# Four graph layers on one core: the written-out order of all engines and the buffer slots replaced by another order of the same steps

## The chip, the cores and the metric

The kernel runs on one core of a Trainium2 chip. The metric is the device time of one execution in microseconds (us), the median of several runs. The core's engines are named as in the profile: PE is TensorE (matmuls; PEld its weight loads), DVE is VectorE, ACT is ScalarE, POOL is GpSimd, SP is SyncE, which here does nothing but issue DMAs. Each has a queue of instructions that it takes strictly in order.

## What is computed

x has 128 batches of 128 nodes with 512 features in float32; adj is one 128 x 128 matrix for all of them. Four layers follow each other, each added to its input and normalised over the features:

```python
x = layernorm(x + (norm_adj @ (x @ W0) + bias))          # layer 0, norm_adj = D^-1/2 adj D^-1/2
x = layernorm(x + L1(x, adj, adj, b))                     # layer 1
q, k, v = x @ Wq.T, x @ Wk.T, x @ Wv.T                    # layer 2
rel = adj.T * (q @ k.T);  rel /= norm(rel, rows)
x = layernorm(x + rel @ v)
h = x @ W3;  e = leaky_relu(h @ a1 + (h @ a2).T) * adj    # layer 3
x = layernorm(x + elu(softmax(e) @ h + beta * h))
```

The kernel has nothing of layer 1 but a normalisation that it joins with that of layer 0.

## The kernel before

**Groups and steps.** The 128 batches are 32 groups of 4 (GB). A group's work is cut into some 240 named steps, methods of the class `Group`; each step issues a few instructions on one engine. A step is written `group.step`, and `s.` stands for the setup of constants and weights. Each of the four large products of a group (w: layer 0's x @ W0; z: layer 2's x times the product Wq.T Wk; v: x @ Wv.T; k: layer 3's x @ W3) is done by seven products of half-size blocks instead of eight (`w1` to `w7`), some of them (1, 2, 5, for v and z also 4) cut once more in the same way. That needs sums of blocks of the left operand (done by POOL) and of the weights (done once by DVE), and additions of the results (DVE).

The steps that the text speaks of:

- `y00` to `y11` (L935): norm_adj times a quarter of x, on TensorE, into a PSUM bank; `cy..` (ACT, L579) copies it to SBUF as y_T. `bi..` (POOL, L585) adds the bias to the same quarter of x in place, after the matmuls that read it.
- `sy0` to `sy3`, `ly12`, `ly5` (POOL, L585): the block sums S_y, l_y of y_T. `w1`, `w2`, ..., `w18` (TensorE, L766 for whole blocks, L730 for those cut once more). `bw`, `ew` (ACT L579, DVE L582): additions inside a cut product. `dw1`... (DVE, L582): results added onto x. `stw`, `gw`, `pow`, `apw`: mean, variance and normalisation.
- `xt`, `nt` (DVE, L674): transposes in 32 x 32 squares of x, for layers 2 and 3. `xd`, `nd` (SP, L680): 16 DMAs that put the squares in their places. `lx12`, `sx0`..., `ln12`, `sn0`... (POOL): block sums of what they bring. `z..`, `v..`, `k..`: the products.
- `r`, `rm`, `sq`, `rp`: rel and its norm. `rt` (DVE) transposes rel by squares, `wr` (SP, L703) writes it to DRAM as d_r, and `cr` (SP, L707) reads it back as relT in four DMAs. `f` (TensorE, L1190) multiplies relT and v, and `fa` (DVE, L1199) adds the result to x.
- `sc` (DVE, L1214), `pw`, `pe` (SP): the attention scores; `pl`, `ej`, `ei`, `ex`, `rd`, `so`: their softmax. `at` (DVE), `aw` (SP, L703, d_a), `cat` (SP, L707, attT) transpose it as above; `h` (TensorE, L1190) multiplies attT and the product k; `em`, `ee`, `ea` do the elu. `qk`, `gk`, `pok`, `apk`: normalisation. `fin` (SP) writes the output; `ld` (SP) loads a group's x.
- Setup: `s.adjt` (TensorE, L822, L823) transposes norm_adj and adj; `s.warm` (TensorE, L833) does 11 transposes of the identity whose result nobody reads; `s.m012_0` and the like (DVE) are sums of weight blocks.

**What sets the order.** Nothing is scheduled by a compiler. The steps are issued in the order of three strings: HEAD (L110 on) once; TURN (L258 on) 14 times, each time with the group numbers one higher, the last group entering with 11 to 24; TAIL (L275 on) once. Inside a turn some five groups are in work at a time. Every engine takes its own instructions in that order, and waits for the other engines and for DMAs by semaphores. An engine that waits holds back all that stands behind it in its queue.

**Buffers.** Each tile with one of nine tags (bank: six PSUM banks; S, l1, l2: block sums; C: products; aT: transposed operands; m: 128 x 512 tiles such as rel, relT, e, attT; x; q) gets the slot that the string SLOTS names for its turn in the list (L47 on, class `Slotted`). A tile waits until all readers of the tile before it in its slot are done.

```python
for base, steps in (
    [(0, HEAD)] + [(g - BACK, TURN) for g in range(FIRST, end, STEP)] + [(end - BACK, TAIL)]
):
    for group, name in (t.split(".") for t in steps.split()):
        todo[group if group == "s" else base + int(group)].step(name)
```

Of the kernel before, what the change touches and what calls it, by code (L numbers as in the profile page):

```python
# [48 lines left out]
        "012345012345013324015345231455124240510435012532245312312023543413421402402052145230142402"  # L49
        "405233100340153013205320521340135305355234252351453524503210430454115310512125312305211451"  # L50
        "412523102304253042541105305015021541030340351405232432352315320142424230314525325435403451"
        "025252541243050250302310324152525234530121521015041053425252503201454254142134120352525210"
        "514323523435403451025252541243050250302310324152525234530121521015041053425252503201454254"
        "142134120352525210514323523435403451025252541243050250302310324152525234530121521015041053"
        "425252503201454254142134120352525210514323523435403451025252541243050250302310324152525234"
        "530121521015041053425252503043201513105140152035033042453510140541524513202020314220445020"
        "545523405212550033235143024014515313210213142055015354151041043201425125523020130023054354"
        "2045151501250312315415401340132145131523152403145324501324051324051"
    ),
    "S": (  # L60
        "012345601326054321502461532143250123654012106425231064104632501462035142560413524651203546"
        "413406524103561463205164231534062135410216534012605403216504352651403256124320651423046145"
        "320641563062145360231534062135410216534012605403216504352651403256124320651423046145320641"
        "563062145360231534062135410216534012631450326154036413652014326504152602324316052432560324"
        "152630645016325064152306"
    ),
    "l1": (
        "010111010101010010101011001101001011010010110100101101001011010010110100101101001011010010"
        "110100110010110011010110100100110"
    ),  # L70
    "l2": (
        "010101010101010010110110110110110110110110110110110110110110110110110110110110110101110101"
        "01"
    ),
    "C": (
        "010101010101011010101011011011011011011011011011011011011011011011011011011011011011011010"
# [3 lines left out]
        "012100212102102012012102012102012102012102012102012102012102012102012102012102102012012010"  # L80
        "2110210"
    ),
    "m": (
        "012301202302301210320100130133212013131201310310213231201012103232120131323021213103232120"
        "131323021213103232120131323021213103232120131323021213103232120131323021213103232120131323"
        "02121310233221302022132020213201210312121203210030"
    ),
    "x": (
        "0123457869789012345768901234576890123457689012345768901234576981032"
    ),  # L90
    "q": (
        "010101010101010001001010101010101010101010101011010101010101010100101010101001010101010101"
        "010101010101010001010101010101010101010101010101010101010101010101010101010101010101010101"
        "010101010101010101010101010101010101010101010101010101010101010101010101010101010101010101"
        "010101010101010101010101010101010101010101010101010101010100010101010101010101010101010101"
        "01010101010101010101010101010101010101010101010101010101010101010101010"
# [14 lines left out]
0.ld1 2.ld0 0.ld0 2.ld1 1.ld1 1.ld0 s.warm s.deg s.root s.nadj s.adjt s.nadjT 0.y10 0.y01 0.cy10  # L111
1.y10 0.cy01 1.y11 1.cy10 1.y01 1.cy11 0.y11 s.m012_0 1.cy01 3.ld1 s.s00 0.w2 s.m012_1 0.cy11
s.s02 0.bi10 s.m012_3 0.y00 0.bi01 2.y10 s.s01 0.cy00 2.y11 0.bi00 0.w1 s.m05_0 0.sy0 s.s03 2.y00
1.y00 0.bi11 s.m05_1 1.cy00 0.sy2 s.m012_2 0.w5 1.bi10 s.m05_3 0.sy3 0.dw1 s.m05_2 0.w6 0.sy1
0.dw2 s.sk0 1.ly12 s.sk2 s.g1 0.dw6 s.s30 0.w7 s.cg1 1.sy0 s.m312_0 1.bi11 0.dw7 s.m312_1 0.w4
1.bi00 0.dw5 s.bi 0.w3 s.sa1 2.cy10 0.dw4 2.cy00 s.sk1 2.cy11 s.g2 s.sa0 0.dw3 0.stw3 3.y11 1.bi01
0.stw0 s.g5 0.stw1 s.sa2 s.dg2 2.y01 s.s31 1.sy2 0.stw2 1.w2 2.cy01 s.s33 s.g6 0.gw s.sa3 1.bw2
s.m35_0 1.w1 s.cg6 0.pow 1.ew2 s.g7 1.bw1 s.m35_1 2.bi11 1.ew1 0.apw0 0.apw1 1.w28 0.xt0 1.ly5
1.w18 s.cg7 s.sk3 s.la 0.apw2 0.apw3 1.sy1 1.w5 1.dw1 3.ld0 0.xt2 s.g4 1.bw5 0.xt1 2.bi01 0.xt3
s.q11 1.w6 2.bi00 s.cg4 0.xd 1.ew5 s.mg12_0 3.bi11 1.w58 s.dg5 s.q02 s.g3 2.bi10 1.dw6 1.dw2 1.w7  # L120
s.dg3 2.ly12 s.mg12_1 1.dw7 s.mg12_3 1.w4 s.sg0 1.dw5 s.sg2 2.w2 s.sg1 4.ld0 2.w1 s.m312_3 2.bw2
s.sg3 2.ew2 2.bw1 0.z1 0.sx0 s.vt3 s.vt0 0.sx2 s.vt1 2.w28 0.cz1 1.dw4 1.sy3 s.vt2 0.z6 1.stw3
s.vd 0.sx1 1.stw2 1.w3 0.cz6 0.sx3 s.mg4_0 2.sy0 0.z5 2.ew1 1.dw3 2.sy1 0.z7 s.mg4_1 2.ly5 1.stw1
2.w18 s.mg4_3 0.cz7 0.z2 2.sy2 0.dz5 1.stw0 0.z4 0.dz2 1.gw s.mg5_0 s.mg12_2 1.pow s.mg5_2 0.z3
0.cz4 s.mg5_1 s.m35_3 1.apw3 s.mg5_3 3.y10 2.dw1 1.apw2 s.sv0 0.v1 1.apw0 3.bi10 2.dw2 1.apw1
1.xt2 s.sv1 0.v2 0.cv1 1.xt3 0.dz3 0.v6 1.xt0 0.dv2 1.xt1 0.r0 s.sv3 0.cv6 1.xd s.mv5_0 2.w5
s.mv4_0 s.mv5_1 s.mv4_1 s.sv2 0.r1 2.bw5 s.mv4_3 s.mv12_0 0.r2 2.ew5 0.r3 s.mv12_2 s.mv12_1 2.w58
s.mv5_3 s.mv12_3 0.rm 0.v7 s.q10 0.sq0 0.rt 0.sq1 2.w6 0.sq2 s.q12 0.cv7 s.q03 0.sq3 s.q00 0.rp
0.v4 s.q13 0.v5 3.cy11 s.q01 3.cy10 0.wr 2.dw6 0.cv4 4.ld1 3.sy0 s.wt0 s.s32 2.w7 2.sy3 0.cr 0.dv5
s.wt1 s.mv5_2 3.y00 1.sx0 2.dw7 0.v3 s.mg4_2 3.cy00 1.lx12 2.dw5 2.w4 s.mv4_2 0.dv3 0.f3 2.dw4  # L130
3.sy1 0.f1 2.stw2 0.f2 3.bi00 2.stw3 1.v1 0.fa3 1.lx4 0.fa2 1.z1 1.bv1 0.fa1 2.w3 1.bz1 1.ev1
1.lx5 1.ez1 0.f0 1.sx2 1.v5 2.dw3 0.fa0 1.z18 1.sx3 1.bv5 2.stw0 1.v18 0.mnv 1.cz1 1.ev5 1.z5
1.sx1 0.qv2 1.z6 2.stw1 0.qv1 1.cv1 0.qv0 1.z2 1.cz6 1.v6 1.bz2 0.qv3 1.ez2 1.bz5 1.z7 0.gv 2.gw
1.ez5 0.pov 1.cv6 2.pow 1.z28 0.apv3 1.z4 1.cz7 1.dz2 0.apv0 1.z58 0.nt3 2.apw0 1.v2 0.sc00 2.apw2
0.nt0 3.y01 1.bz4 0.sc01 0.apv2 1.v58 3.bi01 1.ez4 3.cy01 1.v7 0.apv1 0.nt2 3.ly5 2.apw1 0.sc10
1.bv2 1.z48 2.apw3 0.nt1 1.v4 1.cv7 3.ly12 1.dz4 0.nd 1.ev2 3.w5 1.bv4 1.dz5 1.v28 3.bw5 0.sc11
1.z3 3.ew5 1.dv2 3.w1 0.sc20 3.w2 1.dz3 3.bw1 0.sc21 3.w58 3.ew1 1.r0 1.r1 0.sc30 3.bw2 1.ev4 1.r2
1.r3 3.ew2 1.v48 0.sc31 3.w18 1.dv4 3.w28 0.pw 3.dw1 1.rm 0.k2 0.sn0 3.dw2 1.sq0 2.xt1 1.sq1 0.sn2
0.pe 2.xt0 0.k1 1.sq2 2.xt2 1.sq3 0.sn3 2.xt3 0.k5 1.rt 0.ck1 2.xd 1.rp 1.dv5 s.m312_2 0.sn1 0.pl3
0.dk2 1.v3 0.pl0 s.m35_2 0.pl1 0.pl2 3.sy2 0.k6 1.dv3 0.ej 3.w6 0.ck6 3.sy3 0.ei 0.ex0 0.k7 3.dw6  # L140
0.ex3 0.ex2 0.ex1 3.w7 0.rd 0.ck7 0.so0 0.dk5 0.so1 4.y11 3.dw7 1.wr 0.k4 3.dw5 4.bi11 0.at 0.aw
2.lx12 3.w4 4.cy11 1.cr 0.ck4 3.w3 3.dw4 2.sx0 3.stw2 0.cat 2.z1 3.stw3 2.sx2 2.z2 3.dw3 2.bz1
3.stw0 1.f2 2.sx1 2.bz2 3.stw1 2.v1 2.lx5 2.ez2 1.f0 3.gw 0.k3 1.fa2 2.bv1 3.pow 1.fa0 2.ez1 1.f1
2.lx4 3.apw0 0.dk3 1.f3 3.apw3 3.xt0 3.apw1 2.z18 1.fa1 3.apw2 0.h0 1.fa3 2.cz1 2.v5 3.xt2 1.mnv
3.xt1 0.h3 1.qv0 2.ev1 2.z28 1.qv1 2.z6 3.xt3 1.qv2 2.dz2 3.xd 1.qv3 0.em3 2.v18 0.em0 2.bv5 1.gv
0.h1 2.cz6 2.ev5 1.pov 0.ee0 2.z7 0.ee3 0.em1 1.apv3 0.ea0 1.apv0 0.ea3 2.v58 2.cz7 2.z5 1.sc00
0.ee1 1.apv1 4.y00 1.sc01 2.bz5 0.ea1 4.y10 1.apv2 4.bi00 2.ez5 4.cy00 4.y01 4.cy10 4.bi10 1.sc10
0.h2 4.cy01 1.sc11 2.z4 4.bi01 2.cv1 0.em2 2.v2 1.sc20 2.bz4 4.sy0 0.ee2 2.z58 2.ez4 2.bv2 2.v6
4.ly12 2.ev2 1.nt1 2.z48 2.cv6 1.sc21 2.v28 2.dz4 2.sx3 2.v7 1.sc30 3.sx0 2.dz5 4.w1 1.sc31 2.cv7
3.lx12 2.dv2 2.z3 1.pw 4.bw1 1.nt2 4.ew1 2.v4 2.dz3 1.pe 4.w18 3.sx2 1.nt0 2.bv4 2.r0 1.nt3 3.lx5  # L150
4.dw1 2.r1 2.ev4 3.z2 4.sy2 0.ea2 2.r2 1.pl3 1.pl0 2.r3 4.sy1 0.mnk 1.pl2 4.w6 1.pl1 3.sx1 2.rm
0.qk3 2.rt 2.sq0 1.ej 2.v48 0.qk2 2.wr 4.dw6 3.z1 2.dv4 1.nd 2.sq1 3.lx4 0.qk1 4.w7 1.ei 2.dv5
3.bz1 1.ex0 3.ez1 1.ex1 2.v3 1.ex3 4.sy3 1.ex2 4.dw7 2.sq2 3.bz2 1.rd 2.sq3 1.so0 3.z18 3.ez2
# [1254 lines left out]
```

## Time and profile before

| what | value |
|---|---|
| median of 3 runs | 1981.98 us (1981.17 to 1983.0) |
| profiled execution | 1983.26 us |
| its span | 1981.5 us, so 1.76 us lie around it |
| granted TensorE clock | 0.998 |
| busy: PE, DVE, POOL, ACT | 1954.1, 1645.2, 1372.1, 1125.0 us |
| first and last matmul | 1.43 and 1969.43 us |
| w0 (first weight) landed | 12.75 us |

How to read the profile: times in the trace are us from the start of the span. A line of the timeline has start, duration, engine, source line and operation, output and inputs, shapes and count; in brackets the idle time before it and what ended it. A line of the waits gives engine and instruction, what it waited for, us in total, times, and the longest. A line of the windows gives the stretch and its length, then busy us and number of instructions of each engine, the granted clock, the busy share of the DMA engines and GB/s. Matmuls are pipelined: a duration of one includes its way through the array, so gaps are measured from start to start.

### The profile page before, as it was taken

The page shows a single profiled execution, that of the slowest core. Times are in us where ns is not written, and L with a number is a line of the kernel's source. Part 1 is how long each engine was busy: PE and PEld are TensorE (multiplying, and loading weights), DVE is VectorE, ACT ScalarE, POOL GpSimd, SP SyncE. Part 2 cuts the span into 40 slices and gives each one's busy share as a digit, 9 for nine tenths or more (in the row PEclk, how much of TensorE's full clock was granted, in tenths as well). Part 3 has the DMA queues.
Part 4 walks back from the last instruction along what each step waited for, and adds up shares of the span by engine and source line. Part 5 has one row for each costly group of instructions (what it writes and reads, how often), then busy time and mean ns, then how long its engine had stood idle before and what let it go on. Part 6 is the DMA issues. An engine that isn't in the chain of part 4 may idle for free.

```text
span 1981.5 us, 37439 instructions
## 1 busy us (share of the span) xinstructions
PE 1954.1 (99%) x12405; PEld 1723.5 (87%) x12405; DVE 1645.2 (83%) x3801; ACT 1125.0 (57%) x2800; POOL 1372.1 (69%) x1702
## 2 busy tenths in 40 slices
PE   8999999999999999999999999999999999999997
PEld 7888988888888988888988888988889888898885
DVE  7888787888788888888888888888888888787887
ACT  2245556565655656565556556556656556566467
POOL 7557678676687776786766776766877767777652
PEclk9999999999999999999999999999999999999999
DMA  5523455334444345444345443445343454434434
GB/s 199 85 52 66 96 80 135 60 87 101 106 100 95 66 89 107 104 99 76 81 91 113 98 106 58 92 98 112 92 102 59 92 106 100 96 62 107 76 73 107
DMA packets 737312, 184.55 MB, mean 93 GB/s; under 512 B 689376, under 2 KB 689760, under 8 KB 737120
## 3 DMA queue, kind: packets, MB, share of 16 engines
q1 hardware_dynamic: 736976, 182.03, 43.7%
q8 instruction: 100, 1.64, 0.4%
q14 instruction: 92, 0.75, 0.1%
q10 hardware_dynamic: 144, 0.13, 0.0%
HBM read 64.03 MB, written 49.87 MB: 57 GB/s over the span
## 4 chain that ended last, share of the span: by engine, by line
PE 86%; SPq 4%; POOL 3%; DMA 2%; DVE 2%; ACT 1%; issue 1%; POOLq 0%; DVEq 0%; ACTq 0%
PE p_w L766 10%; PE p_k L766 10%; PE p_v L730 9%; PE p_z L730 8%; PE p_v L766 8%; PE p_z L766 8%; PE p_w L730 7%; PE p_k L730 6%; PE pr L1142 5%; PE pl_k L1190 5%; PE pl_v L1190 5%; PE py L935 5%; SPq L680 4%; POOL x L585 1%; PE pk L1059 1%
## 5 line engine op out<-in xcount | busy, mean ns | idle before, releaser
L1029 ACT ACTIVATE x<-x,nb,r 128x512 f32<-128x512 f32 x383 | 289.6, 808 | 28.8 <-POOL nb L585 28.5
L585 POOL TENSOR_TENSOR x<-x,bias_bc 128x512 f32<-128x512 f32 x128 | 165.7, 1299 | 122.0 <-PE py L935 92.3
L588 POOL TENSOR_TENSOR r<-v,minus_half 128x4 f32<-128x4 f32 (+1 forms) x99 | 99.1, 1001 | 200.8 <-ACT v L1025 189.5
L582 DVE TENSOR_TENSOR x<-p_w,x 128x512 f32<-128x512 f32 x224 | 153.6, 686 | 48.4 <-PE p_w L766 22.3
L1214 DVE SCALAR_TENSOR_TENSOR e<-x,wa_bc 128x512 f32<-128x512 f32 x256 | 172.3, 673 | 1.4 <-ACT x L1029 0.7
L579 ACT COPY C_k<-p_k 128x512 f32<-128x512 f32 x124 | 71.7, 579 | 150.0 <-PE p_k L766 137.5
L935 PE MATMUL py<-nadjT,x 128*128 128x128 f32 x1024 | 134.8, 277 | 1.0 <-DVE x L1310 0.6
L935 PEld LDWEIGHTS py<-nadjT,x 128*128 128x128 f32 x1024 | 126.9, 193 | 5.1 <-issue 1.4
L1190 PE MATMUL pl_k<-C_k,attT 128*128 128x512 f32 x248 | 122.9, 594 | 1.8 <-DMA attT<-d_a 1.7
L1190 PE MATMUL pl_v<-C_v,relT 128*128 128x512 f32 x248 | 121.0, 593 | 0.9 <-DMA relT<-d_r 0.9
L766 PE MATMUL p_z<-S_x,gq 128*128 128x256 f32 x512 | 121.3, 380 | 0.2 <-DVE C_z L582 0.2
L766 PE MATMUL p_w<-w,S_y 128*128 128x256 f32 x512 | 121.2, 379 | 0.4 <-DVE x L582 0.4
L766 PE MATMUL p_v<-wvT,S_x 128*128 128x256 f32 x512 | 121.1, 379 | 0.0
L1305 ACT ACTIVATE pl_k<-pl_k 128x512 f32<-128x512 f32 x127 | 73.4, 581 | 80.3 <-DVE x L1302 79.4
L766 PE MATMUL p_k<-w,S_n 128*128 128x256 f32 x496 | 117.3, 379 | 0.0
L1199 DVE SCALAR_TENSOR_TENSOR x<-pl_v,r,x 128x512 f32<-128x512 f32 x128 | 94.7, 746 | 23.9 <-PE pl_v L1190 18.9
L582 DVE TENSOR_TENSOR p_z<-p_z,q_z 128x128 f32<-128x128 f32 x248 | 107.3, 433 | 8.5
L582 DVE TENSOR_TENSOR p_v<-p_v,q_v 128x128 f32<-128x128 f32 x248 | 107.3, 433 | 8.5
L766 PEld LDWEIGHTS p_z<-S_x,gq 128*128 128x128 f32 x512 | 94.2, 190 | 21.2 <-issue 6.9
L582 DVE TENSOR_TENSOR C_v<-p_v,C_v 128x512 f32<-128x512 f32 x127 | 86.5, 681 | 28.9 <-ACT C_v L579 13.5
L766 PEld LDWEIGHTS p_w<-w,S_y 128*128 128x128 f32 x512 | 93.2, 190 | 12.2 <-issue 1.1
L766 PEld LDWEIGHTS p_k<-w,S_n 128*128 128x128 f32 x496 | 91.6, 190 | 14.0 <-issue 2.9
(1627 smaller groups left out, 6246.6 us busy)
## 6 DMA issues: line engine op xcount, KB each, us to landing
x<-in_x_dram SPq DMA_DIRECT2D x64, 512.0 KB, 4.5
out_dram<-x SPq DMA_DIRECT2D x127, 256.0 KB, 2.5
d_r<-ru SPq DMA_DIRECT2D x31, 256.0 KB, 2.0
relT<-d_r SPq DMA_DIRECT2D x124, 64.0 KB, 2.5
s<-d_s SPq DMA_DIRECT2D x31, 256.0 KB, 3.8
d_a<-au SPq DMA_DIRECT2D x31, 256.0 KB, 2.3
attT<-d_a SPq DMA_DIRECT2D x124, 64.0 KB, 4.0
w<-in_L_gnn_weight_dram SPq DMA_DIRECT2D x1, 1024.0 KB, 9.5
```

What stands on the lines that cost most here:

```text
L582: nc.vector.tensor_tensor(o, a, b, f)
L585: nc.gpsimd.tensor_tensor(o, a, b, f)
L588: nc.gpsimd.tensor_tensor(o, v, minus_half[:, : v.shape[-1]], ALU.pow)
L680: nc.sync.dma_start(out=o[rows(to), :, :, rows(q)], in_=self.u[rows(q), :, :, to])
L730: nc.tensor.matmul(self.banks[i][:, r, bass.ts(c, P)], lhsT=lhsT, rhs=rhs, start=(not then and n == 0), stop=(n == len(steps) - 1), skip_g ...
L766: nc.tensor.matmul(ps[:, j, :], lhsT=lhsT, rhs=rhs, start=(i not in ONTO and j == 0 and kc == 0), stop=(j == 1 and kc == 1), skip_group_ch ...
L935: nc.tensor.matmul(o, lhsT=self.x_chunk(b, kc), rhs=nadjT, start=True, stop=True)
L1029: nc.scalar.activation(xt, xt, AF.Identity, bias=self.nb[k][:, b : b + 1], scale=self.rstd[k][:, b : b + 1],)
L1142: nc.tensor.matmul(self.pr[:, b, :], lhsT=self.whole["z"][:, fc, b // 2, bass.ts(b % 2, P)], rhs=self.xT.chunk(b, fc), start=(fc == 0), st ...
L1190: nc.tensor.matmul(ps, lhsT=left[:, b, :], rhs=self.whole[k][:, b, :], start=True, stop=True)
L1199: nc.vector.scalar_tensor_tensor(xt, self.pf[b], self.rnorm[:, b : b + 1], xt, ALU.mult, ALU.add, accum_out=self.total("v", b),)
L1214: nc.vector.scalar_tensor_tensor(wide(self.e), self.x(b), 1.0, wide(wa_bc[k]), ALU.mult, ALU.mult, accum_out=self.s[:, k, b : b + 1],)
```

## The change

Only the strings change: SLOTS, HEAD, TURN and TAIL. HEAD, TURN and TAIL hold 2333, 240 and 2040 steps after, 2332, 240 and 2041 before; over the whole program each step occurs as often as before, 7733 in all. No function changes. The order of steps is another one in many places on all five queues. Cut to the places that the text speaks of:

```diff
 HEAD = """
-0.ld1 2.ld0 0.ld0 2.ld1 1.ld1 1.ld0 s.warm s.deg s.root s.nadj s.adjt s.nadjT 0.y10 0.y01 0.cy10
-1.y10 0.cy01 1.y11 1.cy10 1.y01 1.cy11 0.y11 s.m012_0 1.cy01 3.ld1 s.s00 0.w2 s.m012_1 0.cy11
+2.ld1 2.ld0 0.ld0 0.ld1 1.ld0 1.ld1 s.deg s.root s.nadj s.adjt s.warm s.nadjT 0.y01 1.y10 0.cy01
+0.y10 1.cy10 1.y11 0.cy10 1.y01 1.cy11 s.m012_0 3.ld1 s.s00 0.w2 1.cy01 s.m012_1 s.s02 0.bi01
...
-2.sc20 3.v48 5.cy11 5.bi11 4.ew5 1.k7 2.nd 5.sy0 3.dv4 2.sc21 4.w58 1.ck7 5.sy1 3.dv5 1.k28 4.dw5
-5.y01 1.ln5 1.dk2 4.w3 4.stw2 5.cy01 4.stw3 5.ly12 3.v3 2.sc30 4.dw3 2.sc31 3.f2 4.stw1 5.bi01
-5.w1 3.dv3 3.f3 3.fa2 5.bw1 4.stw0 3.f1 3.fa3 1.k5 4.gw 2.pw 5.ew1 4.pow 3.f0 1.bk5 3.fa1 5.w2
-2.ln12 4.apw3 3.fa0 2.pe 5.w18 4.apw0 1.ek5 1.cat 1.k4 3.mnv 5.bw2 4.xt3 3.qv0 5.ew2 2.sn0 1.k58
-3.qv3 2.k1 5.dw1 1.ck4 1.sn3 1.dk5 2.pl3 5.w28 2.pl1 4.xt0 2.k2 3.qv1 5.sy2 5.dw2 1.k3 3.qv2 2.sn1
+4.dw3 2.apv1 2.nt3 3.v3 1.ck7 2.nt2 2.nt1 2.sc01 1.k5 2.nt0 5.y11 1.bk5 1.at 3.cr 2.nd 3.f2 1.ek5
+5.cy11 5.bi11 3.f3 3.fa2 5.sy0 1.k58 3.dv3 3.fa3 3.f0 5.sy1 1.dk5 3.f1 2.sc10 1.k4 3.fa0 2.sc11
+4.stw0 5.y01 1.ck4 2.sc20 5.cy01 5.bi01 4.stw1 2.sc21 4.gw 5.ly12 3.fa1 2.sc30 3.mnv 3.qv0 1.aw
+2.sc31 3.qv3 4.pow 2.pw 5.w1 3.qv1 2.ln12 4.apw0 5.w2 4.apw1 2.pe 4.xt0 1.cat 3.qv2 4.xt1 5.bw2
+3.gv 2.sn0 5.ew2 4.apw2 2.k1 5.bw1 4.apw3 4.xt2 1.sn3 5.w28 2.bk1 5.ew1 2.k2 2.pl3 2.sn2 2.pl1
+2.ek1 1.k3 2.pl2 2.bk2 2.pl0 2.sn1 2.ek2 1.h2 5.sy2 1.dk3 5.w18 4.xt3 3.pov 1.h0 1.em2 4.xd 5.dw1
...
 TURN = """
-4.w1 3.xd 2.cv7 0.qk1 4.w2 4.ly5 2.dv4 4.bw1 1.k1 2.dv5 0.qk3 4.ew1 1.k2 4.bw2 0.gk 1.pl0 0.pok
+4.w1 3.xd 0.qk3 2.dv4 4.ly5 4.w2 4.bw1 2.dv5 0.qk1 1.k1 4.ew1 4.bw2 2.v3 0.gk 0.pok 4.ew2 1.bk1
...
-4.w5 1.aw 2.fa2 5.ld0 4.w7 5.ld1 4.bw5 2.mnv 3.sx0 4.ew5 2.qv0 1.cat 3.z1 2.qv2 4.dw7 3.sx1 4.w58
+2.qv1 1.rd 5.ld1 4.ew5 5.ld0 4.w7 2.qv3 1.ck6 1.so0 2.gv 3.z1 4.dw7 2.pov 4.w58 3.bz1 1.so1 4.w4
+3.ez1 2.apv3 2.apv2 2.nt3 3.sx0 2.apv1 3.z18 1.at 2.apv0 1.k7 4.dw5 3.sx1 1.aw 3.cz1 2.nt1 2.nt0
+3.sx2 1.k28 4.dw4 1.ck7 4.w3 2.nt2 3.lx5 1.cat 1.dk5 1.dk2 1.k4 4.stw2 3.sx3 4.dw3 2.nd 3.lx4
...
```

## Prediction

> **What bounds the kernel now.** I read the page first, then TensorE's waits, then windows of 62 us, then the timeline where the order changes.
>
> ```profile
> span 1981.5 us, 37439 instructions
> ...
> PE 1954.1 (99%) x12405; PEld 1723.5 (87%) x12405; DVE 1645.2 (83%) x3801; ACT 1125.0 (57%) x2800; POOL 1372.1 (69%) x1702
> ...
> PE   8999999999999999999999999999999999999997
> ```
>
> TensorE is full in all slices but the first and the last. Its matmuls start every 111, 216 or 429 ns (128, 256 or 512 columns); all 12405 at that pitch come to 1937.7 us. The first starts at 1.43, the last at 1969.43: 30 us of holes, and a tail of 12. The change keeps every step, so 1937.7 stays; only holes can change.
>
> ```profile
> core 0: us, PE busy (x) PEld busy (x) DVE busy (x) ACT busy (x) POOL busy (x), PEclk, DMA share, GB/s
> ...
> 186.00:248.00 62.00, 62.00 (x429) 57.19 (x428) 48.37 (x111) 31.50 (x88) 42.52 (x53) 1.00 0.35 82
> 248.00:310.00 62.00, 61.22 (x369) 51.91 (x368) 54.24 (x133) 33.86 (x82) 49.55 (x66) 1.00 0.53 103
> 867.00:928.00 61.00, 61.00 (x399) 54.28 (x398) 51.69 (x120) 36.16 (x92) 44.14 (x57) 1.00 0.45 94
> ```
>
> By start-to-start gaps the holes are 11.9 us before 62, 3.1 in the next window, 1.3 and 0.2 in the two after; from 560 to 1700 there are none (a turn takes 60.07 us, its matmuls at pitch 60.2 by my count). So the steady turn has nothing to give; whatever the change gains lies in HEAD and TAIL. The waits name the removable part:
>
> ```profile
> PE p_w L766 <- DVE x L582: 3.8, 4, 1.7
> PE pl_k L1190 <- DMA attT<-d_a: 1.7, 2, 1.4
> ...
> PE p_z L766 <- DMA x_0T<-sq_x: 1.2, 1, 1.2
> PE pl_v L1190 <- DMA relT<-d_r: 0.9, 1, 0.9
> ```
>
> **Gains: the landings.** In starts, the attT waits are 1.6 us (489.0, group 5) and 0.5 (551.2, group 6). At 470.8 to 481.9 SP issues the 16 DMAs of n_6T, group 5's d_a write is issued only at 482.0 though its data was ready at 480.0, and h waits until 490.7. The new order gives group 5 10.6 us from `at` to `h` by its list (8.0 before), and group 6's d_a no longer stands behind squares: -2.1. By the same count n_0T gets 13.1 us instead of 11.35 (needed: 13.3, below): -0.5 of 0.7; relT of group 0 6.8 instead of 6.1: -0.7 of 1.1; x_0T 6.6 instead of 5.9: -0.6 of 1.4. Together **-3.9**. The holes from 290 to 348 (2.7, on POOL, DVE and banks) are reordered: between 0 and -2.7, I take **-1.3**.
>
> **Price 1: the entry to group 5's w product.** This is the large term.
>
> ```profile
> 244.08 11.64 SPq L680 DMA_DIRECT2D n_2T<-sq_n  x16
> ...
> 246.90 1.06 PE L935 MATMUL py<-nadjT,x 128*128 128x128 f32 x8
> ...
> 248.89 1.42 POOL L585 TENSOR_TENSOR l_y<-y_5T 128x256 f32<-128x256 f32 x2
> ...
> 250.26 0.73 POOL L585 TENSOR_TENSOR l_y<-l_y,y_5T 128x256 f32<-128x256 f32 x1
> ...
> 252.33 0.61 PE L730 MATMUL p_w<-m,l_y 128*128 128x128 f32 x4
> ...
> 257.42 1.42 POOL L585 TENSOR_TENSOR l_n<-n_2T 128x256 f32<-128x256 f32 x2 [1.54 <-DMA d_s<-s]
> ```
>
> Step 5.y01 is the matmuls at 246.90; copy, l_y on POOL, then 5.w1 at 252.1, with 4.3 us of other matmuls between. In the new HEAD `5.y01` and `5.w1` are neighbours on TensorE (lead 0; in the turn 13.4), and on POOL bias 5.bi01 stands ahead of 5.ly12. The second matmul of w1 needs the third l_y: y01 1.06, semaphore 0.1, bias 1.27 (as at 251.76), l_y 1.42 and 0.73, so 4.5 us after y01's start, against 1.0 unstalled: **3.5 late**.
>
> Then 2.k1. In the list before, 14.9 us of matmuls lie between 2.nd and it; now 8.5. The row says what is needed: first of 16 issues at 244.08, l_n at 257.42, 13.3 us. Laying the new list's matmuls end to end (list time; trace time is about 43 more), nd can start at 207.3 when the last transpose is done, l_n at 220.6, its third operation ends at 222.8, and k1's second matmul has its place at 216.9: 5.9 late. Behind these three l_n operations POOL has 2.sn0 (1.28) and then 1.sn3 (1.29), for which 1.k3 waits: 222.8 + 2.6 and the handovers give 226.0, place 219.1: **6.9 late**. The three are nested: each absorbs the lateness of the one before. Price +6.9; from 6 to 8 if it all stands, 0 if that work would have been late anyway (rival B).
>
> **Price 2: the start.**
>
> ```profile
> 1.43 2.61 PE L833 MATMUL pt_warm<-ident 128*128 128x128 f32 x11 [1.43 <-POOL ident masks.py:199]
> ...
> 5.64 6.95 PE L935 MATMUL py<-nadjT,x 128*128 128x128 f32 x48 [0.45 <-DVE nadjT L826]
> 12.86 1.32 PE L766 MATMUL p_w<-w,y_0T 128*128 128x256 f32 x5 [0.28 <-DMA w<-in_L_gnn_weight_dram]
> ```
>
> The 11 warming transposes lay in dead time; now they follow the two transposes of nadj, so y starts at 4.98 + 11 x 0.213 = 7.3, not 5.64, and five blocks (4.5 us at full speed) instead of six precede the first w product, which w0's landing holds to 12.8. Does warming pay there? The row: after all transposes y still ran at 213 ns a matmul until 8.15, 2.5 us, 1.25 of it lost. [...] I take the row: 0.2 late, and 0.9 for the sixth block done later. DVE is 97% busy from 12.75 to 70 and sets the pace there, so about half is hidden: **+0.5** (0 to 2.4).
>
> DVE's own order: three sums of weight blocks (2 to 4.6 us) now stand before the work for 0.z1, where before they came after. TensorE already waits for DVE in this stretch: **+1.5** (0 to 3).
>
> **Price 3: small leads.** `4.z6` stands directly behind `4.z18` (copy 0.59, handover 0.27), and some bank and sum leads in HEAD fall: **+1.5** (0 to 4, no row of before shows them). Tail: neighbours are exchanged, both signs, 1 us; 0.
>
> **The turn**, run 14 times. SP's order there changes: loads of group 5 stand before d_a instead of between d_a and attT. Shortest new leads: relT to f 6.8 us, needed 5.1 (four issues 2.6, landing 2.5); squares to l_n 12.8 against 13.3, but k1 has 10 us more; s to pl 4.4. All hold by list: 0, and each 0.1 missed costs 1.4.
>
> **Sum.** -3.9 - 1.3 + 6.9 + 0.5 + 1.5 + 1.5 = +5.2. The profiled execution took 1983.26 (span 1981.5 and 1.76 around it), 1.3 above the median, so I put the sum on the median: 1981.98 + 5.2, about **1987.0**.
>
> **Rivals.** A, the forecast: 1984.5 to 1989.5, 0.47.
> B, on the other side: the 6.9 is a loan. In 186 to 248 TensorE has no hole but POOL and DVE are behind it, and the 2.7 us of holes at 290 to 348 show that they would have stopped it soon; then standing still at 258 only lets them catch up, and the landings' 3.9 and the start's prices remain: 1981.98 - 3.9 - 2.7 + 2.5 = 1978. It decides if the late work refills within one turn. For it: DVE at 54 of 62 us after 248. Against: 2.7 of holes can repay at most 2.7 of 6.9. 0.15.
> C: in addition the turn gets a wait. One of 0.3 us, 14 times, is 4.2: 1991. For it: SP's new order and the lead of 6.8. Against: slack of 1.7 there. 0.11.
> D: the price is half as large (POOL reaches 5.bi01 early, or squares start before 207.3), so that gains and prices cancel: 3.5 instead of 6.9 gives 1983.6; with the small leads at 0, 1982 to 1983. That the landings were corrected and nothing else matters falls here. 0.27.
>
> 0.2% is 4.0 us, about what a measurement of this kernel can tell from no change: under 1978.0 faster, over 1986.0 slower. Of A 0.41 lies above, of C 0.11; of B nearly all lies below: slower 0.52, faster 0.14, same 0.34. The range leaves out B's lower end and C's upper, and reaches over D and A: 1980.5 to 1992.5.
>
> **What would show it.** TensorE waits at p_w for l_y near 258 and at p_k for l_n, then S_n, soon after; their sum 6 to 8. No wait of pl_k for attT near 490 and 551. The first py at 7.3. Windows from 560 to 1700 full. If the window 248 to 310 is as full as before, price 1 is wrong; if the turns are over 60.1 us, C holds.

## The result, and the profile after

The changed kernel took 1990.92 us (median of 5 runs, 1989.78 to 1992.29), the one before 1981.98 (5 runs): ratio 1.0046, 95% interval 1.0031 to 1.0060, so 6 to 12 us slower. Its profiled execution took 1991.07 with a span of 1989.3; that of before 1983.26 and 1981.5. The traces therefore differ by 7.8 us, and these are accounted for below.

The page after, beside the rows shown of before: the busy times of the engines are nearly the same, only the span is longer.

```profile
span 1989.3 us, 37384 instructions
...
PE 1955.8 (98%) x12405; PEld 1725.7 (87%) x12405; DVE 1639.1 (82%) x3801; ACT 1130.1 (57%) x2800; POOL 1368.5 (69%) x1702
```

Two of the three windows after. The turn (867 to 928) is full as before; in 248 to 310 TensorE is busy 56.33 us instead of 61.22, and its granted clock is 0.94 instead of 1.00, which is new:

```profile
core 0: us, PE busy (x) PEld busy (x) DVE busy (x) ACT busy (x) POOL busy (x), PEclk, DMA share, GB/s
248.00:310.00 62.00, 56.33 (x321) 48.47 (x320) 53.66 (x129) 34.48 (x80) 43.24 (x55) 0.94 0.51 92
867.00:928.00 61.00, 61.00 (x397) 54.25 (x396) 50.09 (x118) 35.60 (x89) 44.00 (x57) 1.00 0.43 91
```

TensorE's waits after. The l_y of POOL, 0.2 us before, leads the list; 3.2 of its 5.8 us stand at the place that was forecast, 2.0 near 56 us:

```profile
PE p_w L730 <- POOL l_y L585: 5.8, 3, 3.2
...
PE p_k L730 <- POOL l_n L585: 1.6, 1, 1.6
PE pl_k L1190 <- DMA attT<-d_a: 1.1, 1, 1.1
...
PE pl_v L1190 <- DMA relT<-d_r: 1.0, 2, 0.6
```

**Where the time came from.** Both programs do the same matmuls, so the two traces can be laid on each other by work done: the time at which TensorE has behind it the same us of matmuls at full pitch (the transposes of the setup left out), after minus before. The last digit of these readings is rough.

| work done | time before | after is later by |
|---|---|---|
| 20 us | 31.1 | -0.2 |
| 60 | 76.3 | 2.6 |
| 140 | 158.6 | 1.2 |
| 230 | 248.5 | 2.8 |
| 260 | 278.9 | 10.5 |
| 350 | 372.0 | 10.7 |
| 550 | 574.8 | 9.2 |
| 1935 | 1961.5 | 8.9 |

After the last matmul it is 10.8 us to the end instead of 12.0, which gives back 1.2. So: 2.6 from the start, of which 1.4 are regained by 140 and 1.6 lost again by 230; 7.8 at one place of 30 us; 1.6 regained after it, and 1.2 at the end. The place is the one that was forecast. TensorE's timeline there after:

```profile
260.04 1.05 PE L935 MATMUL py<-nadjT,x 128*128 128x128 f32 x8
260.93 0.39 PE L730 MATMUL p_w<-w,y_5T 128*128 128x128 f32 x2
264.55 0.71 PE L730 MATMUL p_w<-m,l_y 128*128 128x128 f32 x4 [3.23 <-POOL l_y L585]
...
266.63 0.63 PE L730 MATMUL p_k<-w,n_2T 128*128 128x128 f32 x2
268.84 1.22 PE L730 MATMUL p_k<-m,l_n 128*128 128x128 f32 x4 [1.58 <-POOL l_n L585]
```

Step 5.y01 starts at 260.04, w1's second matmul at 264.55: 4.5 us later, as worked out. But compare the durations: four matmuls with l_y show 0.71 at 264.55, four with l_n 1.22 at 268.84. Between these the clock fell. A view of short windows shows it best (last columns: granted clock, DMA share, GB/s):

```profile
261.00:264.50 3.50, 0.32 (x3) 0.12 (x2) 3.27 (x10) 2.41 (x8) 3.32 (x4) 1.00 0.64 91
264.50:265.50 1.00, 0.95 (x8) 0.95 (x9) 0.00 (x0) 0.97 (x3) 0.93 (x2) 1.00 0.83 208
265.50:268.80 3.30, 1.76 (x10) 1.47 (x9) 1.36 (x2) 2.49 (x7) 3.07 (x5) 0.54 0.17 52
268.80:272.00 3.20, 3.16 (x13) 2.92 (x14) 2.82 (x9) 3.20 (x10) 3.14 (x3) 0.50 0.83 151
272.00:276.00 4.00, 4.00 (x22) 3.32 (x22) 2.99 (x9) 1.27 (x4) 4.00 (x5) 0.93 0.01 2
```

TensorE stands still for 3.4 us, works at full speed for 1.2, and then gets half the clock from 265.7 to 272.6, 6.8 us, although it has work for all of that time but the second wait of 1.9. Half the clock for the other 4.9 us costs some 2.5, and 3.4 + 1.9 + 2.5 makes the 7.8.

### The profile page after: what moved, and what is told of

It is laid out like the page before. It is cut to its first block, busy times and chain, and to the rows that moved or that the text cites. A ratio compares the mean times of both kernels' runs of the same rounds, so it can differ in the third digit from the quotient of the medians.

```text
span 1989.3 us, 37384 instructions
## 1 busy us (share of the span) xinstructions
PE 1955.8 (98%) x12405; PEld 1725.7 (87%) x12405; DVE 1639.1 (82%) x3801; ACT 1130.1 (57%) x2800; POOL 1368.5 (69%) x1702
## 4 chain that ended last, share of the span: by engine, by line
PE 92%; DVE 2%; SPq 2%; DMA 1%; POOL 1%; ACT 1%; issue 0%; DVEq 0%; POOLq 0%; ACTq 0%
PE p_k L766 11%; PE p_w L766 10%; PE p_z L730 9%; PE p_v L730 9%; PE p_v L766 9%; PE p_z L766 8%; PE p_k L730 7%; PE p_w L730 7%; PE pr L1142 6%; PE pl_v L1190 5%; PE pl_k L1190 5%; PE py L935 5%; DMA a_bc<-in_L_gnn_a_dram 1%; SPq L680 1%; PE pk L1059 0%
## 5 line engine op out<-in xcount | busy, mean ns | idle before, releaser
L579 ACT COPY C_z<-p_z 128x512 f32<-128x512 f32 x97 | 56.3, 580 | 97.3 <-PE p_z L766 89.7
L579 ACT COPY q_z<-p_z 128x256 f32<-128x256 f32 x124 | 45.9, 370 | 115.2 <-PE p_z L730 106.3
L766 PEld LDWEIGHTS p_v<-wvT,S_x 128*128 128x128 f32 x512 | 93.3, 190 | 13.7 <-issue 2.2
```

The lines of the kernel that those rows point to most:

```text
L579: nc.scalar.copy(o, i)
L766: nc.tensor.matmul(ps[:, j, :], lhsT=lhsT, rhs=rhs, start=(i not in ONTO and j == 0 and kc == 0), stop=(j == 1 and kc == 1), skip_group_ch ...
```

## The experiments

Theory: the change pays at one place for a lead that its list lacks (l_y, then l_n behind it, nested), and for standing still with half a clock; the start costs something more; the landings give back little. Rivals: the wait is a loan that other engines pay back; the waits add up instead of nesting; the clock has nothing to do with them; the landings are late by traffic and not by the queue. "Before" and "changed" below name the two kernels; ratios are to the kernel before, run in the same session. Each trace is of one execution.

**1. The place alone, put into the kernel before** (b_y01). HEAD of before (two bank slots are exchanged with it):

```diff
-5.y01 1.ln5 1.dk2 4.w3 4.stw2 5.cy01 4.stw3 5.ly12 3.v3 2.sc30 4.dw3 2.sc31 3.f2 4.stw1 5.bi01 5.w1
+1.ln5 1.dk2 4.w3 4.stw2 4.stw3 3.v3 2.sc30 4.dw3 2.sc31 3.f2 4.stw1 5.y01 5.cy01 5.bi01 5.ly12 5.w1
```

> The kernel before with one thing of the change: 5.y01 stands directly ahead of 5.w1 on TensorE, and 5.bi01 ahead of 5.ly12 on POOL. Theory (the place costs what its lead lacks): w1's second matmul waits 3.4 us for l_y near 255, and TensorE's granted clock falls to about 0.5 for 3 to 7 us after it, which costs 1.5 to 3 more; 2.k1 has lead enough not to wait. Time +5 (1985.5 to 1988.5). Rival (a loan): POOL and DVE catch up meanwhile, and the holes from 290 to 348, 2.7 us in the kernel before, are gone: +1 to +2.5.

Measured: 1986.51, ratio 1.0020 (1.0011 to 1.0029), +3.9. In its trace TensorE is 0.7 early at 225 us of work, 6.0 late at 245 and 5.2 at 300: in this execution one missing lead costs 6.7, of which 0.8 are paid back. The wait itself is half of it:

```profile
255.37 1.23 PE L730 MATMUL p_w<-m,l_y 128*128 128x128 f32 x4 [3.22 <-POOL l_y L585]
...
256.82 3.62 PE L1190 MATMUL pl_v<-C_v,relT 128*128 128x512 f32 x4
```

Four matmuls of 512 columns take 3.62 us; at full clock the same row is 1.88 before. The price is no loan: 5.6 us of it are there at 1935. The traced execution, 1988.88 us at a mean granted clock of 0.996, is the second slowest of 11; the two at 0.998 took 1984.91 and 1985.41, and the trace of the kernel before, also at 0.998, has full clock all the way from 8.1 to 1974.2 us. So by estimate from these times the wait alone costs some 2.5 us, and the half clock, where it falls, as much again or more.

**2. The place repaired for w1 only** (a_y01). The changed HEAD, with y01 in another free bank:

```diff
-3.dv5 2.apv3 1.k7 2.sc00 2.apv2 4.dw3 2.apv1 2.nt3 3.v3 1.ck7 2.nt2
+3.dv5 2.apv3 1.k7 5.y01 2.sc00 2.apv2 4.dw3 2.apv1 2.nt3 3.v3 1.ck7 5.cy01 5.bi01 5.ly12 2.nt2
```

> The changed kernel with 5.y01, 5.bi01 and 5.ly12 moved some 10 us of TensorE work earlier. Theory (nested waits): w1 waits no more, but the squares of n_2T are issued when they were, so 2.k1 now waits 5 us instead of 1.9 for l_n, the clock falls after it as it did, and the time stays within 1 us (1990 to 1991). Rival (the waits add up): -3.4 and the clock stays full after 1.9 us: -6, 1985.

Measured: 1992.42, ratio 1.0049 (1.0035 to 1.0063): nothing gained. w1 runs through, its 3.4 us stop is gone, and 2.k1 takes all of it back:

```profile
261.48 0.39 PE L730 MATMUL p_w<-w,l_y 128*128 128x128 f32 x2
264.77 0.46 PE L730 MATMUL p_k<-w,n_2T 128*128 128x128 f32 x2 [2.90 <-DMA n_2T<-sq_n]
266.91 1.23 PE L730 MATMUL p_k<-m,l_n 128*128 128x128 f32 x4 [1.68 <-POOL l_n L585]
```

2.90 and 1.68 us, and half clock (1.23 for four matmuls) with the second. The waits are nested: the squares of n_2T and the sums behind them set the price, whether or not w1 waits.

**3. TensorE kept working through both waits** (a_busy). The first matmul of each of the two products is done again and again, into the same place with the same values:

```diff
+BUSY = {("w_5", 1): 14, ("k_2", 1): 11}
-            for n, (r, c, a, b) in enumerate(steps):
+            again = 0 if then else BUSY.get((self.name, i), 0)
+            for n, (r, c, a, b) in enumerate(steps[:1] * again + steps):
+                n = max(0, n - again)
```

> The changed kernel with the first matmul of w1 of group 5 repeated 14 times and that of k1 of group 2 repeated 11 times, into the same place with the same result, so that TensorE works through both waits instead of standing still. Theory (the half clock is the price of standing still for 3.4 us): granted clock 1.0 from 261 to 277; l_n and S_n still come when they come, so that of some 2.5 us at half clock only about 1 is gained: 1990. Rival (the clock would have fallen anyway): matmuls at 213 ns from 265.8 as before, 1991 or later.

Measured: 1990.25, ratio 1.0035 (1.0023 to 1.0048). The clock does not fall:

```profile
262.00:266.00 4.00, 3.87 (x34) 3.68 (x34) 0.86 (x4) 3.11 (x8) 3.71 (x7) 1.00 0.48 108
266.00:268.00 2.00, 2.00 (x20) 2.00 (x19) 1.71 (x3) 2.00 (x6) 1.92 (x3) 1.00 0.65 100
268.00:270.00 2.00, 1.31 (x12) 1.15 (x11) 1.93 (x5) 2.00 (x5) 2.00 (x3) 1.00 0.99 162
```

Without the repeated work, TensorE passes the place 0.9 us less late than in the changed kernel: 6.9 instead of 7.8. So here it is standing still that takes the clock (0.50 from 265.7 to 272.6 in the changed kernel, 1.00 with the repeated work), and of the some 2.5 us that the half clock costs only 0.9 are gained, since l_n and the sums behind it come no earlier. It could not have been earlier: S_n for 1.k3, the last of the three nested terms of the forecast, ends at 270.65, just ahead of the product that reads it:

```profile
269.36 1.29 POOL L586 TENSOR_TENSOR S_n<-n_1T,S_n 128x512 f32<-128x512 f32 x1
270.71 1.99 PE L769 MATMUL p_k<-w,S_n 128*128 128x256 f32 x8
```

**4. The start: single parts undone in the changed kernel.** a_sums moves eight sums of weight blocks behind 0.z7; a_ly2 moves `2.ly12` ahead of `2.bi01`; a_warm moves `s.warm` ahead of `s.deg`.

> The changed kernel with its eight early sums of weight blocks for g and layer 3 (mg5, mg4, m35) put behind 0.z7 on DVE, as they mostly stood in the kernel before. Theory (DVE sets the pace from 45 to 70): the 2.9 us by which TensorE is later there than in the kernel before shrink by 2 to 3: 1988.5. Rival (POOL's l_y and the bias of groups 1 to 3 set it): within 0.7: 1990.5.

> The changed kernel with 2.ly12 ahead of 2.bi01, 2.bi10 and 3.bi11 on POOL (three biases of 1.27 us and more each), since TensorE waits 2.15 us at 56.3 for that l_y: the new order asks for 2.w2 before 1.w7 and 1.w4, the one before after them. Theory (the early loss of 2.7 us is POOL's l_y): no wait at 56, TensorE 1.5 to 2.5 earlier at 100: 1989. Rival (DVE sets the pace there): other waits grow by as much, within 0.5: 1990.7.

> The changed kernel with the 11 warming transposes back ahead of the transposes of norm_adj. Theory (the start is set by the landing of w0 and then by DVE): y starts at 5.6 instead of 7.3, TensorE stands before w0 or later for DVE, and is no earlier at 30: 1990.9 within 0.5. Rival (the transposes cost what they last): 1.5 to 2 earlier for good: 1989.2.

Measured: a_sums 1991.18 (ratio 1.0039, 1.0026 to 1.0053), a_ly2 1990.99 (1.0044, 1.0031 to 1.0056), a_warm 1990.80 (1.0041, 1.0028 to 1.0053): none differs from the changed kernel (1.0046) by more than the intervals. That one of these three parts carries the start's loss finds no support. In a_ly2 the wait for l_y at 56 is gone, and one for DVE stands 3 us further on in its place:

```profile
61.02 1.99 PE L766 MATMUL p_w<-w,S_y 128*128 128x256 f32 x8 [1.54 <-DVE x L582]
```

In a_warm y began at 6.57 (its x landed only then) and the first w product at 13.31, no earlier than the 12.93 of the changed kernel.

**5. The whole start of before** (h_start): the first 305 steps of HEAD of before, then all other steps in the changed order, with slots assigned again where lifetimes overlapped.

> The first 305 steps of HEAD in the order of before (TensorE's first 66 us of work, to about 80 us), all later steps in the changed order. Theory (the start loses 2 to 6 us, and differently in each execution): in the five traces whose start is that of the change TensorE reaches 60 us of work at 78.2 to 82.9, in the three with the start of before at 76.3 to 76.6; with that start -2.5 to -4: 1987.5, and the times lie closer together. Rival (the start is hidden, as DVE and POOL catch up by 100): within 1 of the changed kernel, 1990.5.

Measured: 1988.83 (1987.98 to 1992.45), ratio 1.0033 (1.0021 to 1.0046): the medians say 2.1 less than the changed kernel, the ratios 2.6, and the intervals overlap. Its trace has TensorE at 60 us of work at 76.3, exactly as before, and 2.1 to 3.0 ahead of the changed kernel from there to 250 us of work; the place then costs 8.4 (from 0.3 late at 230 to 8.7 at 250). So by the traces the start loses about 2.6 us as a whole order, and none of the parts tried alone; by time this is not shown. It also varies: at 60 us of work the four traces that start as the changed kernel does are 1.8 to 6.5 late, the five others that start as before does -0.5 to 1.3.

**6. The clock at the start** (a_keep). In one execution of a kernel with the changed start (a_split), z's product waits three times as long at 68 as in the changed kernel's own trace, and runs on half clock shortly after. Its row at 71.14 is still at full speed for the first half; 73.44 is the next product, 3.07 us where 1.89 is usual:

```profile
66.21 1.89 PE L768 MATMUL p_z<-x_0T,gq 128*128 128x256 f32 x8
71.14 2.52 PE L768 MATMUL p_z<-S_x,gq_t 128*128 128x256 f32 x8 [3.04 <-DVE x L583]
73.44 3.07 PE L768 MATMUL p_w<-w,S_y 128*128 128x256 f32 x8
```

a_keep fills the two waits at 23 and 67 with repeated work (`AGAIN = {"2.y00": 3, "0.z1": 2}`).

> The changed kernel with 2.y00 done three times and 0.z1 twice on TensorE, into the same places with the same result: 1.8 and 1.7 us of work in the two stretches, at 23 and 67, where TensorE waits 1.1 to 3.2 us for DVE. Theory (a wait of some 3 us there halves the clock for the next 3 to 7 us in some executions, which makes the start's loss vary): no matmuls at 213 ns after 20 us, TensorE at 60 us of work by 78 to 79 (without the repeats), times 0.5 to 1.5 lower and closer together. Rival (the clock plays no part in the start): later by up to the 3.5 us of added work.

Measured: 1992.16 (1991.05 to 1994.05), ratio 1.0050 (1.0036 to 1.0063). In its trace the clock is 1.00 from 20 to 34 and from 56 to 80 us, but nothing is gained (at the place its clock is at half for 10.2 us, against 6.8 in the changed kernel's trace). Half a clock at the start is something that some executions have (the mean clock is 0.83 in a_sums and 0.84 in h_both from 20 to 30 us, 0.86 in a_split from 56 to 80); that it makes the median's loss is not shown. Why DVE is 1 to 2 us later there in some executions stays open.

**7. The trains on SP's queue** (a_split, b_split). The 16 DMAs of one transposed square are issued in two parts, and the write of d_r or d_a between them:

```diff
-            for q in range(4):
-                for to in range(4):
-                    nc.sync.dma_start(out=o[rows(to), :, :, rows(q)], in_=self.u[rows(q), :, :, to])
+            for q, to in [(q, to) for q in range(4) for to in range(4)][part]:
+                nc.sync.dma_start(out=o[rows(to), :, :, rows(q)], in_=self.u[rows(q), :, :, to])
```

> The changed kernel with three trains of 16 DMAs for squares cut in two, so that the write of d_r or d_a that stands behind the train is issued when its data is ready: x_2T after 2 (before d_r of group 1), n_1T after 5 (d_r of group 2), n_6T after 13 (d_a of group 5). Theory (a train of 11 us on SP's queue is what these transfers wait for): the waits for relT at 162 and 223 and for attT at 501 go, 0.5 + 0.7 + 1.2 = 2.4 us: 1988.5. Rival (the landing itself is late, because the squares' packets share the DMA engines): d_r and d_a land as late as before, no gain: 1990.7.

> The kernel before, otherwise unchanged, with two trains cut in the same way: n_6T after 13 (d_a of group 5) and n_7T after 5 (d_a of group 6). Theory: the waits of h for attT at 489 and 551 go, 1.6 + 0.5: 2 us faster than before, 1980. Rival as for the changed kernel: no gain, 1982, or the rest of the squares comes late and l_n waits for it: +1.

Measured: a_split 1992.21 (1.0043, 1.0029 to 1.0056), b_split 1981.65 (0.9996, 0.9987 to 1.0005): by time neither can be told from its parent. By trace, b_split is 1.7 us earlier at 1935 us of work; the two waits for attT are gone. In a_split the wait for relT at 162 is gone, that at 224 is 0.4 instead of 0.7, and that of group 5 for attT 0.6 instead of 1.2; from 100 to 1935 us of work it gains 1.5, not 2.4. In the traces the queue was the cause for most of these waits; the rest of a cut train still holds back the four reads behind it.

**8. Both orders joined** (h_both, h_both_split): before's first 1294 steps, to about 345 us, then the changed order; the second also cuts n_6T after 13.

> The first 1294 steps of HEAD in the order of before (to about 345 us), all later steps, TURN and TAIL in the changed order. Theory (the change loses all it loses before 345 and gains after: attT 1.2 to 1.6, turns 0.4, the end after the last matmul 1.2): 2 to 3 us faster than before, 1979.5. Rival (those gains exist only because TensorE came late): 1982.

> As h_both, and the train of n_6T cut after 13 of its 16 DMAs, so that d_a of group 5 is issued when it is ready. Theory: h of group 5, which waits about 1.2 us for attT in the changed order, waits 0 to 0.6: 1978.7. Rival (the landing of attT is late by the squares' traffic, whatever its place in the queue): as h_both.

Measured: h_both 1981.14 (0.9993, 0.9985 to 1.0002), h_both_split 1980.29 (0.9990, 0.9981 to 0.9999), against 1982.61 for before in that session. By time the first can't be told from before; the second is the fastest, by 0.2 to 3.8 us. d_a now goes out inside the train, 2.6 us ahead of its end:

```profile
472.62 8.93 SPq L679 DMA_DIRECT2D n_6T<-sq_n  x13
481.67 0.55 SPq L705 DMA_DIRECT2D d_a<-au  x1
482.26 1.98 SPq L679 DMA_DIRECT2D n_6T<-sq_n  x3
```

Three traces agree on what the change gains after 345 us: 2.9 in the changed kernel's own (10.7 late at 350 us of work, 7.8 at the end), 2.1 in that of h_both (from 1.0 late at 345 to 1.1 early at the end) and 2.8 in that of h_both_split (from 0.9 to 3.7 early, part of it by the cut train). It is less than a third of the 10.7 that is lost before.

## Why the prediction was right, and where its sizes were off

It forecast 1987.0 and "slower" as likeliest; measured 1990.9. Direction, place and mechanism held; the sum, +5.2, was 2.6 short of the traces' 7.8, and 3.7 short of the medians. The measured time lies 1.4 above rival A's own 1984.5 to 1989.5 and inside the whole range only because that reaches up to C; it is C's number, 1991, without C's cause. The measured terms below add up to the 7.8. The terms that fell short make 4.2 together: 0.9 in price 1, 1.2 in the start, 0.6 in attT and 1.5 in the holes after 290; gains of 1.5 in turn and tail, which were put at 0, hide part of it.

- **Price 1, +6.9: measured +7.8.** The l_y wait was put at 3.5 and took 3.4; l_n was to bring the lateness to 5.9, and the second wait of 1.9 and some matmuls at half speed do that; S_n's wait never showed, since slowed matmuls let POOL come first. The missing term is the clock: the working priced the waits and not what standing still does to the matmuls after it. With the clock kept up the place costs 6.9, the size as worked out, and S_n is ready only then (experiment 3). Nested, as claimed (experiment 2).
- **Price 2 with the x_0T gain, +2.0 - 0.6: measured +2.6.** The first y at 7.29 (7.3 forecast), y at 213 ns until 9.63 (the row's 2.5 us: 2.3) and the first w product at 12.93 (7.3 + 4.5 + 1.25, so 13.0) came as worked out, and this part was paid back by 31 us. In part this was luck: y's full clock came at 9.75 here, but at 7.55 in a_split's trace, with y starting at 7.25 as well; the stretch of 3.4 us before it held 3.1 us of work there, all but two matmuls of it transposes. So in that trace full clock followed work that was nearly all transposes; when it comes differs from execution to execution. The +1.5 for the sums was the wrong cause: what shows at 56 is `2.w2`, which the change asks for ahead of 1.w7 and 1.w4, waiting 2.15 us for POOL's l_y. Taking either away alone gains nothing in the times; in the traces the loss goes with the whole order, and no single cause of it is shown (experiments 4 and 5).
- **Landings of relT and n_0T (-1.2) and small leads (+1.5): measured +0.2 from 60 to 230 us of work.** Gains of 1.4 to 140, then waits of f for relT at 162 (0.5) and 223 (0.7) and smaller ones. These are trains again: d_r of group 2, ready at 208.3, is issued at 216.7 behind n_1T's 16 DMAs; before it was issued first, at 201.4. In part the change moved the blocked place from attT to relT.
- **attT, -2.1: measured -1.5 from 350 to 550 us of work,** of which the two waits for attT make 0.9 and one for S_x at 547, now gone, 0.4. Group 6's wait of 0.5 is gone. Group 5's 1.6 is still 1.2: the lead by the list grew as computed, but au was ready at 491.4 and d_a still went out behind n_6T, at 493.65. The step counted TensorE's lead and left out that SP's order at this spot had not changed.
- **290 to 348, -1.3: measured +0.2.** The holes moved and did not shrink.
- **The turn 0 and the tail 0: measured -0.3 and -1.2.** Rival C, a wait in the turn, is out: windows there are as full as before.
- Rival B (a loan) is out by experiment 1; D (price half as large) is out by the trace.
- Two counts of the prediction are rough, without effect on the sum: in the steady turns of before the matmuls of 128 columns start every 111.5 ns on average, not 111, so all of them come to 1943 us and the holes to some 25, not 30; and DVE is busy 96% from 12.75 to 70, not 97.

## What to carry to other kernels

When a hand-written order leaves one engine without a spare product, work out the whole chain behind the first wait, since the longest of nested waits sets the price and repairing the first one gained nothing here. A stop of TensorE of 3.4 us cost up to twice its length here (6.7 in b_y01's trace), because matmuls ran at half clock after it (3.62 us for four that took 1.88 before); since a stop of 2.15 us was followed by half clock in one trace and by full clock in another, one trace does not give its price (next section). On SP's queue a train of 16 small DMAs, some 11 us long, was a wait for every transfer behind it (d_r of group 2, ready at 208.3, was issued at 216.7): cut the train where the next transfer's data comes ready.

## What the runs showed of the hardware that was not expected

In the changed kernel's trace the clock is full from 9.75 to 265.75 us, half to 272.58 and full to 1982.65; in that of the kernel before it is full from 8.14 to 1974.22. These stretches of 256.00, 6.83, 1710.08 and 1966.08 us are 75, 2, 501 and 576 times 3.413. Half clock after a stop lasted 3.4 us in a_sums (26.4 to 29.8), 6.8 in the changed kernel and in b_y01 (254.65 to 261.5), and 10.2 in a_keep (263.0 to 273.3). What followed a stop differed. The same stop of 2.15 us, for l_y at 56, in the changed kernel's own trace and in a_split's, each line 3.41 us long and a whole number of these from a change of the clock:

```profile
54.12:57.54 3.42, 2.46 (x16) 2.09 (x14) 3.39 (x6) 0.00 (x0) 3.42 (x4) 1.00 0.55 85
57.54:60.95 3.41, 2.38 (x18) 2.30 (x19) 3.41 (x7) 0.75 (x2) 2.04 (x2) 1.00 0.68 96
...
55.34:58.75 3.41, 1.41 (x12) 1.21 (x11) 3.41 (x7) 0.00 (x0) 3.33 (x4) 1.00 0.65 97
58.75:62.16 3.41, 3.41 (x17) 3.23 (x16) 3.34 (x8) 0.74 (x2) 0.73 (x1) 0.50 0.68 97
```

In the first trace the stop is shared by two lines, which hold 2.46 and 2.38 us of work, and the clock stays at 1.00. In the second it lies in one line, which holds 1.41 us of work, and the next line is at 0.50. Cut in the same way, the traces of the kernel before and the changed one have a single stretch at full clock between start and tail that half clock followed: the one with the least work, 1.20 us (262.34 to 265.75, changed kernel). The next lowest, 1.78 us (23.40 to 26.82, changed kernel), was followed by full clock. The half clock from 265.75 went on after 1.83 us of work in its first 3.41 us and ended after 3.42 in its second. After its stop of 3.4 us the changed kernel ran 1.2 us at full speed before the clock fell at 265.75; in b_y01 it fell at 254.65, 0.7 us before work began again; and a stop of 3.0 us at 23 was followed by half clock in a_sums and not in a_split. (Stops are given from start to start of matmuls, less the pitch; busy times are the profile's, whose ends of matmuls are modelled.)
